# One transpose instead of four for a block's softmax shifts, spread over the query tiles by VectorE with a table

## The chip, the cores and the metric

The kernel runs on one core of a Trainium2 chip. The time is device microseconds of one execution. The kernel before ran three times: 1567.17, 1567.2 and 1570.7 us, median 1567.2. One more execution was profiled: 1566.48 us, with a span of 1564.7 us from the first to the last instruction and a granted TensorE clock of 0.998.

Engine names: PE is TensorE (PEld its weight loads), DVE is VectorE, ACT is ScalarE, POOL is GpSimd, SP issues most DMAs.

## What is computed

A parallel transformer block over `x` of shape (2, 1024, 1024) in float32: the input, plus causal attention with linear position biases, plus a linear layer with binarized weights, both on the normalized input.

```
xn = layernorm(x)
q, k, v = split(clip(xn @ Wqkv.T, -8, 8));  q, k = layer_norm(q), layer_norm(k)   # with weight and bias
scores = q k^T / sqrt(32) + slope[h] * (key_pos - query_pos),  causal mask         # 32 heads of 32
attn = softmax(scores) v @ Wout.T
ffn  = xn @ (mean|W| * sign(W)).T + bias
out  = x + attn + ffn
```

## The kernel before

**Blocks of attention.** The unit of attention is a block (b, qb, g): one of two batches, one of two halves of 512 queries (NQ = 4 tiles of 128), one of eight groups of G = 4 heads. That makes 32 blocks. The four heads of a group lie on partitions 0, 32, 64 and 96 on, so four matmuls, one for each 32 rows of the array, run side by side.

**Two passes over the scores.** The first pass (`first_scores`, L1015 to L1053) has queries on the partitions and finds each query's maximum: matmul L1024, then on VectorE L1043, which adds the position table `rel` and reduces to a maximum; a short instruction on the same line reads the accumulated maximum into `mx` and frees the bank. The second pass (`second_scores`, L1075) has keys on the partitions, because its output is the stationary side of the product with the values. Its exponent needs minus the maximum of each query, which now lies along the free dimension. So the maxima have to be turned.

**Turning the shifts** (`shifts`, L1055 to L1073). `mx` is [128 queries of a tile, 4 heads, 4 query tiles]. GpSimd adds the positions (L1059), negates (L1060) and splits the f32 value into three bf16 parts (L1063, L1065): seven operations of 128x16. They are written into `shift_b`, four tiles of [128, 128], in which head j's three parts stand in columns 32j to 32j+2 of the tile. One step later TensorE transposes the four tiles into one bank (L1070), and ScalarE copies that bank out as `rows` (L1072), [128, 512] in bf16: three rows for each head, 512 queries along them. In `second_scores` a second matmul, here called the fold (L1099), adds the rows to the scores: its stationary operand is three rows of ones, its moving operand the three rows of shifts.

After the fold VectorE masks the diagonal (L1118), ScalarE takes the exponential (L1127), GpSimd adds up the parts for the denominator (L1156), and one step later `weigh_values` multiplies by the values (L1167).

**PSUM.** One pool of seven banks (tag `s`) is used in rotation by everything: first scores, second scores, the turned shifts, projections, transposes and denominators. A new user waits until the reader of the bank seven allocations before is done. An eighth bank holds the attention output.

**The rest of the work** is a generator of pieces: projections of k, q and v by a scheme with seven products for eight (`seven`, L411, with evictions by `combine`, L442 and L453 on VectorE, L458 on ScalarE), the binarized layer (L808, eviction L794), the output projection. Between them, side tasks normalize, transpose (L519) and evict (L585 and L546 on ScalarE).

**The order** is written out: the program issues instructions in the order of the main loop (L1249), and each engine runs its queue in that order. Step n does: `first_scores(n)`; the GpSimd half of `shifts` if a block closes; sometimes `divide`; some pieces; `weigh_values` of step n - 10; `second_scores` of step n - 9; then the second half of the shifts of the block that closed one step before; then more pieces. How many pieces a step takes is computed from fixed costs (`time_of`, `share`, `each`), which know nothing of the shifts.

Of the kernel before, what the change touches and what calls it, by code (L numbers as in the profile page):

```python
# [8 lines left out]
FP = mybir.dt.float32  # L9
FR = mybir.dt.float32r  # L10
BF = mybir.dt.bfloat16
AF = mybir.ActivationFunctionType
ALU = mybir.AluOpType
AX = mybir.AxisListType
# [11 lines left out]
def parallel_block_kernel(  # L26
# [36 lines left out]
    nc = tc.nc  # L63
    B, S, D = x.shape
    P = 128
# [4 lines left out]
    G = 4  # L70
    NQB = S // HALF
    NQ = HALF // P
# [12 lines left out]
    const = ctx.enter_context(tc.tile_pool(name="const", bufs=1))  # L85
# [6 lines left out]
    ps_s = ctx.enter_context(tc.tile_pool(name="ps_s", bufs=7, space=bass.MemoryType.PSUM))  # L92
# [6 lines left out]
    ident = const.tile([P, P], FP, tag="ident", name="ident")  # L99
    make_identity(nc, ident)  # L100
    ident_b = const.tile([P, P], BF, tag="ident_b", name="ident_b")
    nc.vector.tensor_copy(ident_b, ident)
    ones_b = const.tile([P, P], BF, tag="ones_b", name="ones_b")
    nc.vector.memset(ones_b, 1.0)
    ones = const.tile([P, HEAD_DIM], FP, tag="ones", name="ones")
    nc.vector.memset(ones, 1.0)
    mean_w = const.tile([P, P], FP, tag="mean_w", name="mean_w")
# [10 lines left out]
    inv_q = const.tile([P, NC], FP, tag="inv_q", name="inv_q")  # L118
    lnp = const.tile([P, 4, NC], FP, tag="lnp", name="lnp")
    lnq = const.tile([P, 2, NC], FP, tag="lnq", name="lnq")  # L120
    shift_b = const.tile([P, NQ, P], BF, tag="shift", name="shift_b")

    def constants():
        for j, src in enumerate((q_w, q_b, k_w, k_b)):
            nc.sync.dma_start(lnp[:, j, :], src)
        yield 0.0

        nc.gpsimd.iota(  # L130
            rel,
            pattern=[[1, S]],
            base=-(S - P),
            channel_multiplier=-1,
            allow_small_or_imprecise_dtypes=True,
        )
        nc.gpsimd.affine_select(
            out=rel,
            in_=rel,
            compare_op=ALU.is_ge,  # L140
            fill=MASKED,
            base=S - P,
            pattern=[[-1, S]],
            channel_multiplier=1,
        )

        nc.gpsimd.memset(behind, 0.0)
        nc.gpsimd.affine_select(
            out=behind,
            in_=behind,  # L150
            compare_op=ALU.is_ge,
            fill=MASKED,
            base=0,
            pattern=[[1, P]],
            channel_multiplier=-1,
        )

        nc.gpsimd.iota(
            pos,
            pattern=[[0, G], [P, NQ]],
            base=-(HALF // 2),
            channel_multiplier=1,
            allow_small_or_imprecise_dtypes=True,
        )

        nc.gpsimd.iota(
            off,  # L170
            pattern=[[P, NO]],
            base=-(NT - NT // NQB) * P - HALF // 2,
            channel_multiplier=1,
            allow_small_or_imprecise_dtypes=True,
        )

        for h in range(N_HEADS):
            if h % 2 == 0:  # L180
                yield 0.0
            nc.gpsimd.tensor_scalar(kpos[:, h, :], off, slopes[h], None, ALU.mult)
            r0 = HEAD_DIM * (h % G)
            nc.gpsimd.memset(
                inv_q[r0 : r0 + HEAD_DIM, h // G : h // G + 1], QK_SCALE / slopes[h]
            )

        for j in range(2):
            nc.vector.tensor_tensor(lnq[:, j, :], lnp[:, j, :], inv_q, ALU.mult)


        nc.gpsimd.memset(shift_b, 0.0)

# [168 lines left out]
    def score_bank(name):  # L364
        return ps_s.tile([P, HALF], FP, tag="s", name=name)
# [4 lines left out]
    def tokens(t):  # L370
        return slice(t * P, (t + 1) * P)
# [683 lines left out]
    def shifts(b, qb, g):  # L1055

        mx = st.pop(("mx", b, qb, g))
        sh = small.tile([P, G, NQ], FP, tag="sh", name=f"sh_{b}_{qb}_{g}", bufs=2)
        nc.gpsimd.tensor_tensor(sh, mx, pos, ALU.add)  # L1059
        nc.gpsimd.tensor_scalar(sh, sh, -1.0, None, ALU.mult)  # L1060
        sb = shift_b.rearrange("p i (j r) -> p j i r", j=G)
        for n in range(3):
            nc.gpsimd.tensor_copy(sb[:, :, :, n], sh)  # L1063
            if n < 2:
                nc.gpsimd.tensor_tensor(sh, sh, sb[:, :, :, n], ALU.subtract)  # L1065
        yield True

        ps = ps_s.tile([P, NQ, P], BF, tag="s", name=f"trs_{b}_{qb}_{g}")
        for i in range(NQ):
            nc.tensor.transpose(ps[:, i, :], shift_b[:, i, :], ident_b)  # L1070
        rows = small.tile([P, HALF], BF, tag="rows", name=f"rows_{b}_{qb}_{g}", bufs=4)
        nc.scalar.copy(rows, ps.rearrange("p i q -> p (i q)"))  # L1072
        st["rows", b, qb, g] = rows  # L1073

    def second_scores(unit):  # L1075
        add_up_parts(st.pop("adds", []))
        name = "{}_{}_{}_{}".format(*unit[0][0], unit[0][1])
        banks = [score_bank(f"s2_{name}_{j}") for j in range(G)]
        c0 = 0
        for block, kt, q0 in unit:  # L1080
            q, k = st[("q",) + block], st[("k",) + block][kt // NQ]
            c1 = c0 + HALF - q0
            for j in range(G):
                r = slice(32 * j, 32 * j + 32)
                nc.tensor.matmul(  # L1085
                    banks[j][:, c0:c1],
                    k[r, tokens(kt % NQ)],
                    q[r, q0:],
                    start=(c0 == 0),
                    stop=False,  # L1090
                )
            c0 = c1
        c0 = 0
        for block, kt, q0 in unit:
            rows = st[("rows",) + block]
            c1 = c0 + HALF - q0
            for j in range(G):
                r = slice(32 * j, 32 * j + 3)
                nc.tensor.matmul(  # L1099
                    banks[j][:, c0:c1],  # L1100
                    ones_b[r, :],
                    rows[r, q0:],
                    start=False,
                    stop=(c1 == HALF or (block, kt, q0) == unit[-1]),
                )
            c0 = c1
        for j in range(G):
            c0, diagonal = 0, []
            for block, kt, q0 in unit:
                if kt >= block[1] * NQ:  # L1110
                    diagonal.append(c0 // P)
                c0 += HALF - q0
            if diagonal:
                at = banks[j].rearrange("p (i q) -> p i q", q=P)
                step = max(diagonal[-1] - diagonal[0], 1)
                at = at[:, diagonal[0] : diagonal[-1] + 1 : step, :]
                mask = behind.unsqueeze(1).to_broadcast([P, len(diagonal), P])
                nc.vector.tensor_tensor(at, at, mask, ALU.add)  # L1118
        parts = []
        for j in range(G):  # L1120
            pT = work.tile([P, HALF], FP, tag="pT", name=f"pT_{name}_{j}", bufs=16)
            c0 = 0
            for n, (block, kt, q0) in enumerate(unit):
                h = block[2] * G + j
                c1 = c0 + HALF - q0
                a = kt - block[1] * NQ + NT - NQ
                nc.scalar.activation(  # L1127
                    pT[:, c0:c1],
                    banks[j][:, c0:c1],
                    AF.Exp,  # L1130
                    bias=kpos[:, h, a : a + 1],
                    scale=slopes[h],
                )
                if j == 0:
                    parts.append((block, kt, q0, []))
                parts[n][3].append(pT[:, c0:c1])
                c0 = c1

        mine = [p for p in parts if p[0] == parts[0][0]]
        waited = st.pop("waiting", [])  # L1140
        st["waiting"] = parts[len(mine) :]
        st["parts", unit[0]] = mine + waited
        if mine[0][1] == 0:
            st[("sum",) + mine[0][0]] = mine[0][3]
            st["adds"] = waited
        else:
            add_up_parts(mine)

    def add_up_parts(parts):

        for block, kt, q0, pT in parts:
            for j in range(G):
                part_sum = st[("sum",) + block][j][:, q0:]
                late = block == blocks[-1] and kt > NT // 2
                eng = nc.vector if late else nc.gpsimd
                eng.tensor_tensor(part_sum, part_sum, pT[j], ALU.add)  # L1156
# [81 lines left out]
    def short_lead(block):  # L1238

        return block[1] == 1 and block[2] == 0  # L1240

    sides.append(constants())
    fill_until(("q", 0))
    for n in range(3):
# [4 lines left out]
    for n in range(steps + 1):  # L1249
# [22 lines left out]
        if 0 <= m < len(second):  # L1272
            second_scores(second[m])
# [62 lines left out]
```

## Time and profile before

| what | value |
|---|---|
| median of three runs | 1567.2 us |
| the profiled execution | 1566.48 us |
| its span | 1564.7 us, clock 0.998 |
| L1070, transposes | 128, mean 221 ns, first at 311.4, last at 1461.3 |
| L1072, ScalarE's copy | 32, 586 to 718 ns |
| L1059, L1060, L1063, L1065 on GpSimd | 32, 32, 96, 64; medians 232, 254, 253, 230 ns |
| L1099, the fold | 768 matmuls, at 512 wide 376 ns |
| L1118, masks | 320; 424 ns at 256 wide, 291 at 128 |

How to read it: the page gives each engine's busy time, then the chain of work that ended last, then groups of instructions by line, engine and operation, with busy time, mean duration of one, and the idle time just before them with what ended it. The timeline lists instructions in order of time: start, duration, engine, line, what it writes and reads; a number in brackets is idle time before it and its releaser. Instructions of one group that follow each other are merged, with x4 for four of them, and their duration is then that of all together.

### The profile page before, as it was taken

The numbers are of one execution on the slowest core, as the hardware profiler recorded it, in microseconds if no ns is written. First come the engines' busy times: TensorE is split into PE (matmuls) and PEld (weight loads), VectorE is DVE, ScalarE is ACT, GpSimd is POOL, SyncE is SP. The second block draws the span as 40 slices with busy tenths as digits, with TensorE's granted clock in tenths as the row PEclk, the third lists the DMA queues.
The fourth block names the chain that finished last, engine by engine and source line by source line (L and its number), as shares of the span: only waits on it lengthen the run. The fifth ranks groups of instructions, "written<-read, shape, count | busy, mean of one in ns | idle before, by whom it ended". The sixth has DMA issues, their size and how long they took to land.

```text
span 1564.7 us, 25362 instructions
## 1 busy us (share of the span) xinstructions
PE 1539.9 (98%) x8452; PEld 678.9 (43%) x8452; DVE 918.8 (59%) x2617; ACT 689.0 (44%) x1427; POOL 969.5 (62%) x1276
## 2 busy tenths in 40 slices
PE   7999999999999999999999999999999999999998
PEld 3444444444444434333333344555655333343333
DVE  7745353767786566656665565666655565565332
ACT  3543331114665645456543365555444343343430
POOL 4473061024674766675676599877788887777661
PEclk9999999999999999999999999999999999999999
DMA  8877354592333754458932377667677233312232
GB/s 303 296 247 264 101 202 154 176 320 83 103 117 96 251 189 149 116 128 250 277 125 106 140 239 232 142 140 164 140 164 204 80 88 95 88 38 65 58 78 54
DMA packets 117426, 244.94 MB, mean 157 GB/s; under 512 B 10544, under 2 KB 50992, under 8 KB 113968
## 3 DMA queue, kind: packets, MB, share of 16 engines
q1 hardware_dynamic: 90912, 148.94, 28.6%
q0 software_dynamic: 26384, 94.38, 23.5%
q8 instruction: 67, 1.10, 0.3%
q14 instruction: 63, 0.52, 0.1%
HBM read 155.47 MB, written 107.74 MB: 168 GB/s over the span
## 4 chain that ended last, share of the span: by engine, by line
PE 89%; DVE 3%; DMA 2%; POOL 2%; ACT 2%; issue 1%; SPq 0%; POOLq 0%; DVEq 0%; ACTq 0%
PE s L1024 10%; PE s L1085 10%; PE o L1167 8%; PE mm_f L808 8%; PE mm_q_t L411 7%; PE mm_o_t L411 7%; PE mm_v_t L411 7%; PE mm_k_t L411 6%; PE mm_q L411 6%; PE mm_o L411 5%; PE mm_v L411 5%; PE mm_k L411 4%; PE den L1186 2%; PE s L1099 2%; PE tr_k L519 1%
## 5 line engine op out<-in xcount | busy, mean ns | idle before, releaser
L1156 POOL TENSOR_TENSOR pT<-pT,pT 128x512 f32<-128x512 f32 (+3 forms) x628 | 578.2, 980 | 173.3 <-ACT pT L1127 152.3
L1127 ACT ACTIVATE pT<-s,kpos 128x512 f32<-128x512 f32 (+3 forms) x768 | 378.4, 590 | 435.7 <-DVE s L1118 259.3
L1043 DVE CUSTOM_DVE_ANT_0 sumss<-s,rel 128x512 f32<-128x512 f32 (+2 forms) x284 | 179.1, 631 | 104.9 <-PE s L1024 72.9
L1085 PE MATMUL s<-qg,kg 32*128 32x512 f32 (+3 forms) x1536 | 183.7, 520 | 0.6 <-DVE mx L1043 0.6
L1024 PE MATMUL s<-kg,qg 32*128 32x512 f32 (+3 forms) x1536 | 179.6, 521 | 0.2
L1167 PE MATMUL o<-pT,vg 128*32 128x512 f32 (+3 forms) x1536 | 155.5, 494 | 1.2 <-ACT pT L1127 1.2
L808 PE MATMUL mm_f<-sg,hl 128*128 128x512 f32 x512 | 127.0, 399 | 2.1 <-DVE mx L1043 2.1
L1085 PEld LDWEIGHTS s<-qg,kg 32*128 32x128 f32 x1536 | 75.9, 183 | 103.4 <-issue 53.9
L1024 PEld LDWEIGHTS s<-kg,qg 32*128 32x128 f32 x1536 | 73.4, 183 | 105.2 <-issue 46.8
L1118 DVE TENSOR_TENSOR s<-s,behind 128x256 f32<-128x256 f32 (+1 forms) x320 | 96.7, 371 | 35.4 <-PE s L1099 35.2
L411 PE MATMUL mm_o_t<-w_o_t,ot 128*128 128x512 f32 x256 | 116.6, 602 | 0.0
L411 PE MATMUL mm_k_t<-w_k_t,xT 128*128 128x512 f32 x224 | 109.4, 613 | 1.2 <-POOL xT L400 0.8
L411 PE MATMUL mm_q_t<-w_q_t,xp 128*128 128x512 f32 x224 | 108.1, 605 | 0.0
L808 PEld LDWEIGHTS mm_f<-sg,hl 128*128 128x128 f32 x512 | 93.5, 188 | 33.0 <-DVE mx L1043 11.7
L411 PE MATMUL mm_v_t<-w_v_t,xp 128*128 128x512 f32 x224 | 106.3, 606 | 0.1
L411 PE MATMUL mm_k<-w_k,xT 128*128 128x512 f32 x192 | 91.3, 612 | 0.3 <-ACT xT L546 0.3
L411 PE MATMUL mm_v<-w_v,xp 128*128 128x512 f32 x192 | 89.6, 604 | 0.0
L411 PE MATMUL mm_q<-w_q,xp 128*128 128x512 f32 x192 | 88.7, 603 | 0.0
L411 PE MATMUL mm_o<-w_o,ot 128*128 128x512 f32 x192 | 87.7, 602 | 0.0
L1167 PEld LDWEIGHTS o<-pT,vg 128*32 128x32 f32 x1536 | 37.2, 108 | 113.2 <-issue 94.9
L1043 DVE CUSTOM_DVE_ANT_0 umss<-s,rel 128x512 f32<-128x512 f32 x100 | 69.2, 692 | 26.9 <-PE s L1024 16.1
L411 PEld LDWEIGHTS mm_o_t<-w_o_t,ot 128*128 128x128 f32 x256 | 46.7, 190 | 62.5 <-issue 52.7
(224 smaller groups left out, 1985.4 us busy)
## 6 DMA issues: line engine op xcount, KB each, us to landing
xp<-xd SPq DMA_DIRECT2D x16, 1792.0 KB, 8.3
kg<-kd SPq DMA_DIRECT2D x48, 256.0 KB, 4.7
vg<-vd SPq DMA_DIRECT2D x48, 256.0 KB, 5.7
wd_ot<-in_wout_t_dram POOLq DMA_DIRECT2D x11, 1024.0 KB, 9.5
xd<-xT POOLq DMA_DIRECT2D x8, 1280.0 KB, 5.6
x<-in_x_dram SPq DMA_DIRECT2D x16, 512.0 KB, 5.8
kd<-kT POOLq DMA_DIRECT2D x16, 512.0 KB, 4.4
qd<-qT POOLq DMA_DIRECT2D x16, 512.0 KB, 3.9
```

Of the source, the lines that this page charges most:

```text
L411: nc.tensor.matmul(ps, pr[:, FACTOR[block], c, :], W[what, block, c], start=(c == 0), stop=(c == NI - 1),)
L519: nc.tensor.transpose(ps[:, j, :], src[:, (c0 + j) * P : (c0 + j + 1) * P], ident)
L808: nc.tensor.matmul(ps, hl[c // NI][:, m % 2, c % NI, :].bitcast(FR), sg[n, c], start=(m == 0), stop=(m == 2 * NC - 1),)
L1024: nc.tensor.matmul(banks[j][:, c0 : c0 + n], q[r, tokens(i - block[1] * NQ)], k[r, :n], start=True, stop=True,)
L1043: nc.vector.tensor_tensor_reduce(out=sums[:, :n], in0=banks[j][:, c0 : c0 + n], in1=rel[:, o0 : o0 + n], scale=1.0, scalar=m if opened els ...
L1085: nc.tensor.matmul(banks[j][:, c0:c1], k[r, tokens(kt % NQ)], q[r, q0:], start=(c0 == 0), stop=False,)
L1099: nc.tensor.matmul(banks[j][:, c0:c1], ones_b[r, :], rows[r, q0:], start=False, stop=(c1 == HALF or (block, kt, q0) == unit[-1]),)
L1118: nc.vector.tensor_tensor(at, at, mask, ALU.add)
L1127: nc.scalar.activation(pT[:, c0:c1], banks[j][:, c0:c1], AF.Exp, bias=kpos[:, h, a : a + 1], scale=slopes[h],)
L1156: eng.tensor_tensor(part_sum, part_sum, pT[j], ALU.add)
L1167: nc.tensor.matmul(po[32 * j : 32 * j + 32, q0:], v[:, kt % NQ, 32 * j : 32 * j + 32], pT[j], start=(kt == 0), stop=(last is not None and ...
L1186: nc.tensor.matmul(ps[32 * j : 32 * j + 32, :], ones, total[j], start=True, stop=True,)
```

## The change

`shift_b` becomes one tile of [128, 128]. In each head's 32 columns it now holds twelve values: the high parts of the four query tiles, then the middle parts, then the low ones. GpSimd does not negate any more, and writes the low part straight from the subtraction, so five operations are left. One transpose turns everything. A row of the result belongs to one query tile: row r of the bank to tile r mod 4. VectorE reads the bank four times over (the tile dimension is broadcast), multiplies by a table `mine_q` of ones and zeros, which keeps in the columns of tile t only the rows of tile t, and writes `rows`. The fold then takes twelve rows and a stationary operand of minus one. `mine_q` is made once from the identity. ScalarE's copy is gone.

```diff
-    ones_b = const.tile([P, P], BF, tag="ones_b", name="ones_b")
-    nc.vector.memset(ones_b, 1.0)
+    minus_b = const.tile([P, P], BF, tag="minus_b", name="minus_b")
+    nc.vector.memset(minus_b, -1.0)
...
-    shift_b = const.tile([P, NQ, P], BF, tag="shift", name="shift_b")
+    shift_b = const.tile([P, P], BF, tag="shift", name="shift_b")
+    mine_q = const.tile([P, NQ], FP, tag="mine_q", name="mine_q")
...
         nc.gpsimd.memset(shift_b, 0.0)
+
+        nc.vector.tensor_reduce(
+            out=mine_q,
+            in_=ident.rearrange("p (c t) -> p t c", t=NQ),
+            op=ALU.add,
+            axis=AX.X,
+        )
...
         sh = small.tile([P, G, NQ], FP, tag="sh", name=f"sh_{b}_{qb}_{g}", bufs=2)
+        sb = shift_b.rearrange("p (j r) -> p j r", j=G)
+        high, mid, low = (sb[:, :, n * NQ : (n + 1) * NQ] for n in range(3))
         nc.gpsimd.tensor_tensor(sh, mx, pos, ALU.add)
-        nc.gpsimd.tensor_scalar(sh, sh, -1.0, None, ALU.mult)
-        sb = shift_b.rearrange("p i (j r) -> p j i r", j=G)
-        for n in range(3):
-            nc.gpsimd.tensor_copy(sb[:, :, :, n], sh)
-            if n < 2:
-                nc.gpsimd.tensor_tensor(sh, sh, sb[:, :, :, n], ALU.subtract)
+        nc.gpsimd.tensor_copy(high, sh)
+        nc.gpsimd.tensor_tensor(sh, sh, high, ALU.subtract)
+        nc.gpsimd.tensor_copy(mid, sh)
+        nc.gpsimd.tensor_tensor(low, sh, mid, ALU.subtract)
         yield True
 
-        ps = ps_s.tile([P, NQ, P], BF, tag="s", name=f"trs_{b}_{qb}_{g}")
-        for i in range(NQ):
-            nc.tensor.transpose(ps[:, i, :], shift_b[:, i, :], ident_b)
+        ps = ps_s.tile([P, P], BF, tag="s", name=f"trs_{b}_{qb}_{g}")
+        nc.tensor.transpose(ps, shift_b, ident_b)
         rows = small.tile([P, HALF], BF, tag="rows", name=f"rows_{b}_{qb}_{g}", bufs=4)
-        nc.scalar.copy(rows, ps.rearrange("p i q -> p (i q)"))
+        nc.vector.tensor_tensor(
+            rows.rearrange("p (t q) -> p t q", q=P),
+            ps.unsqueeze(1).to_broadcast([P, NQ, P]),
+            mine_q.unsqueeze(2).to_broadcast([P, NQ, P]),
+            ALU.mult,
+        )
...
-                r = slice(32 * j, 32 * j + 3)
+                r = slice(32 * j, 32 * j + 3 * NQ)
                 nc.tensor.matmul(
                     banks[j][:, c0:c1],
-                    ones_b[r, :],
+                    minus_b[r, :],
                     rows[r, q0:],
```

## The prediction

> **What bounds the kernel.** I read the engine shares first, then the chain of work that ended last, then the groups with different shapes kept apart, and last the timeline around each of the 32 places where a block's shifts are turned.
>
> ```profile
> PE 1539.9 (98%) x8452; PEld 678.9 (43%) x8452; DVE 918.8 (59%) x2617; ACT 689.0 (44%) x1427; POOL 969.5 (62%) x1276
> ...
> PE 89%; DVE 3%; DMA 2%; POOL 2%; ACT 2%; issue 1%; SPq 0%; POOLq 0%; DVEq 0%; ACTq 0%
> ```
>
> TensorE is busy for 98% of the span and makes up 89% of the chain. So only TensorE time counts, and other engines count where TensorE waits for them. A busy TensorE also hides short waits, because matmul ends are modelled, so a share alone decides nothing; each place has to be looked at.
>
> The rows that the change touches or resembles (busy us, mean ns of one, idle before):
>
> ```profile
> L1118 DVE TENSOR_TENSOR s<-s,behind 128x256 f32<-128x256 f32 x192 | 68.3, 424 | 24.7 <-PE s L1099 24.6
> ...
> L1072 ACT COPY rows<-trs 128x512 bf16<-128x512 bf16 x32 | 20.1, 627 | 16.3 <-PE trs L1070 16.3
> ...
> L442 DVE TENSOR_TENSOR u_o<-mm_o_t,u_o 128x512 f32<-128x512 f32 x24 | 16.6, 692 | 61.5 <-PE mm_o_t L411 61.5
> ...
> L1070 PE MATMUL trs<-ident_b,shift_b 128*128 128x128 bf16 x128 | 12.7, 221 | 2.1 <-POOL shift_b L1063 2.1
> ...
> L1060 POOL TENSOR_SCALAR sh<-sh 128x16 f32<-128x16 f32 x32 | 8.1, 253 | 2.9
> ```
>
> **TensorE: 96 transposes fewer.** Each block loses three of its four transposes. A record lasts 221 ns, but records overlap: the timeline shows the four together in 0.40 us, so three steps and one record make 0.40, and a step is (0.40 - 0.22) / 3 = 0.06 us. The starts say it more closely: at 1274.85 the first begins, at 1275.08 the matmul behind the four, so 0.23 / 4 = 0.057. I take 0.056, so 0.17 us a block and 96 x 0.056 = 5.4 us in all. That is the upper end from this edit: it counts only where what comes next isn't waiting for something else.
>
> The Trainium skill, page "TensorE: Matmul & The Clock Gate", section on the PE-mode transpose, gives about 275 ns for a bf16 128x128 transpose within a kernel. By it the edit would remove 96 x 275 ns = 26.4 us, an estimate; the steps of 57 ns between starts say that a train of transposes doesn't pay that each, so the sum doesn't use it.
>
> **Where the 0.17 us survives.** I went through the blocks by the time of their first transpose (us from the span's start).
>
> First, the matmul behind the transposes writes the next of seven rotating score banks, which is free only after VectorE has read the third head's row maximum from it (L1043).
>
> ```profile
> 1274.85 0.40 PE L1070 MATMUL trs<-ident_b,shift_b 128*128 128x128 bf16 x4
> 1274.94 0.08 DVE L1043 DVE_READ_ACCUMULATOR2_ANT mx<- 128x1 f32 x1
> ...
> 1275.08 0.69 PE L411 MATMUL mm_o_t<-w_o_t,ot 128*128 128x512 f32 x1
> ```
> ```profile
> 1325.62 0.40 PE L1070 MATMUL trs<-ident_b,shift_b 128*128 128x128 bf16 x4
> ...
> 1325.90 0.08 DVE L1043 DVE_READ_ACCUMULATOR2_ANT mx<- 128x1 f32 x1
> 1326.03 0.30 PEld L411 LDWEIGHTS mm_o_t<-w_o_t,ot 128*128 128x128 f32 x2 [0.19 <-DVE mx L1043]
> ```
>
> In the second the load says that it waits for VectorE; the read ends at 1325.98 and the matmul starts about 0.06 later. In the first there is no wait, but the read ends at 1275.02 and the matmul starts at 1275.08, the same 0.06 behind: both limits coincide. Transposes that end sooner gain nothing in either. The maxima that VectorE is working through were started by L1024, ahead of the transposes, so they do not move. Such blocks: waiting at 357, 984, 1000, 1024, 1040, 1064, 1326, 1420; just touching at 1080, 1180, 1275, 1369. Twelve blocks, gain 0. At 311 the matmul waits 0.28 us for ScalarE's copy of the bank before (L458): gain 0 too.
>
> Second, in the early half little fill stands between the transposes and the next first_scores, which wants the banks that ScalarE's exponentials have yet to read:
>
> ```profile
> 535.27 3.03 ACT L1127 ACTIVATE pT<-s,kpos 128x384 f32<-128x384 f32 x8 [2.66 <-DVE s L1118]
> ...
> 537.21 0.70 PEld L1024 LDWEIGHTS s<-kg,qg 32*128 32x128 f32 x6 [0.76 <-ACT pT L1127]
> ...
> 538.35 0.29 PEld L1024 LDWEIGHTS s<-kg,qg 32*128 32x128 f32 x2 [0.44 <-ACT pT L1127]
> ```
>
> The exponentials end at 538.30 and the last loads go at 538.35. They were released by folds and masks that come before the transposes, and the removed copy (L1072) stands behind them, so nothing here moves. Such blocks: 377, 423, 451, 469, 535, 586, 645, 696, 755, 806, 865, 915. Their eight or sixteen first_scores matmuls take 0.06 to 1.4 us longer from first to last start than the shortest of the same shape (0.55 and 0.77). I give all twelve 0; in the three with 0.06 (645, 696, 865) the wait is there already, so an earlier start only lengthens it.
>
> Free: 328, 406, 941, 1135, 1461. Five x 0.17 = **0.85 us**.
>
> **GpSimd: seven operations become five.** The negation (L1060) and the last cast go. Starts in the train are 0.29 to 0.34 us apart; at 958.20 the seven begin and end at 960.34; with two fewer they end 0.64 us sooner. It matters where TensorE waits for them:
>
> ```profile
> 960.09 0.25 POOL L1063 CAST shift_b<-sh 128x16 bf16<-128x16 f32 x1
> ...
> 960.40 0.40 PE L1070 MATMUL trs<-ident_b,shift_b 128*128 128x128 bf16 x4 [1.52 <-POOL shift_b L1063]
> ```
>
> At 960 the wait falls from 1.52 to about 0.9, and nothing is late behind it: 0.64 + 0.17 = **0.81 us**. At 1232 the wait of 0.6 goes, but then the bank of the first case binds: its read ended at 1231.40, so the matmul starts at 1231.46 instead of 1231.92: **0.46 us**. Elsewhere GpSimd is 3 to 16 us ahead of the transposes. The other 30 blocks relieve it of 0.64 each with nobody waiting: taken as 0.
>
> **VectorE: a product more.** 512 elements out of PSUM with an SBUF table: no row has just this, with bf16 in and out. L442 (692 ns) is nearest; L1118 grows from 291 (128 wide) to 424 (256 wide), which carried on gives an estimate of 690 for 512. I take 0.69 us; the ends are ScalarE's 0.59 for the shortest copy of the same tile and 1.0 for the one cast to bf16 of the start (L102, 998 ns). 32 x 0.69 = 22 us on an engine at 59%. It stands in the queue behind the masks (L1118) and ahead of the next eviction. Queued behind it are that eviction and the next maxima, and TensorE waits for the banks they free. What hides it:
>
> ```profile
> 1135.54 1.42 DVE L1118 TENSOR_TENSOR s<-s,behind 128x256 f32<-128x256 f32 x4
> 1139.20 0.69 DVE L794 TENSOR_TENSOR fo<-mm_f,alpha_bias 128x512 f32<-128x512 f32 x1 [2.24 <-PE mm_f L808]
> ```
>
> VectorE is idle 2.24 us right where the product goes; at the other places from 984 on this gap is 1.55 to 6.3 us, and in most early blocks an idle stretch of 0.7 us or more follows after a few instructions. The wait for the transposes is no new one: they run before the masks end. Packed are 311, 328 and 755: between 0 and 0.69 each if the cover is gone, at most 2.1 us. I take 0: their next bank waits have other releasers (exponentials, ScalarE's copies).
>
> **ScalarE: a copy less.** 20 us go, but the copy stood behind the exponentials and ahead of work with slack. Where ScalarE has no idle stretch behind it (451, 469) up to 0.63 each could come back: 0 to 1.3 us, taken 0. The rows themselves are wanted two steps later or more, so either engine is in time.
>
> **The fold with twelve rows.** No row has twelve. A bf16 weight load of 3 rows takes 93 ns (L1099), of 128 rows 97 ns (L1070), and the 512-wide f32 matmul takes 613 ns with 128 rows (L411) and 640 with 32 (L1085): the row count doesn't set the time. Taken 0; the upper end is 4 ns for each of 768 loads, four side by side, 0.8 us; no reason for a gain. The table mine_q is one VectorE operation near 39 us; 0 taken, 1.0 at most (the cast's 998 ns).
>
> **Sum.** 0.85 + 0.81 + 0.46 = 2.1 us. The profiled execution took 1566.48 (span 1564.7), so 1564.4 of it; it lies 0.7 under the median 1567.2, and from the median I get **1565.1**. A measurement of this kernel tells about 0.3% (4.7 us) from no change.
>
> **Rivals.** (1) All of it comes through: banks and exponentials move up because VectorE's and ScalarE's queues shift too. 5.4 + 2 x 0.64 = 6.7, so 1560.5. For it: TensorE is the bound over the whole; against it: the twenty-five coinciding waits above. (2) Slower: the product delays VectorE's evictions and maxima, and the seven banks come free 0.69 late. It decides where less than 0.69 us of idle time lies between the masks and the next reader of a bank that TensorE wants; if that were so in half the blocks, 16 x 0.69 = 11.0 less 2.1 gives 1576. For it: TensorE's loads waited for L1043 more often than for any other VectorE work, and 357 to 469 and 755 are dense; against it: the gaps shown. (3) Each transpose costs its whole record, as in a train that cannot overlap: 96 x 0.221 = 21 us, 1546. The overlapping starts speak against it.
> By the 275 ns of the Trainium skill (same page and section) this third one would be 1541, an estimate; the trace's steps of 57 ns disagree.
>
> **Numbers.** Forecast 0.68 (all of it within 0.3%), rival 1 0.18, rival 2 0.12, rival 3 0.02. Faster 0.20, within 0.3% 0.68, slower 0.12. The range takes rival 1 and ScalarE's 1.3 below (1559), and above the packed VectorE places, fold and table (2.1 + 0.8 + 1.0) with some of the 3.5 us by which the runs of before differ: 1571.
>
> **What would show it.** Right: the matmul behind the single transpose starts 0.06 after L1043's third read in the twelve blocks; first_scores still ends with the exponentials; the wait at 960 falls to about 0.9 and that at 1232 goes; VectorE's new row reads 0.69 with idle time behind it. Wrong: L442 or L1043 late after the product with TensorE waiting for it, a fold over 376 ns at 512 wide, or a product well over 0.69.

## The result and the profile after

The changed kernel takes 1562.33 us (median of seven runs, 1557.92 to 1564.13), the kernel before beside it 1567.32 us (seven runs, 1566.36 to 1571.02). The ratio is 0.9957, with a 95% interval of 0.9941 to 0.9972: 0.43% faster, about 5 us, where 2.1 us were forecast. The time lies in the range. The likeliest case, a change within 0.3%, did not come (the interval runs from 0.28% to 0.59% faster), and the experiments below show that the larger part of the gain comes from places that the prediction priced at nothing.

The profiled execution took 1562.7 us, with a span of 1560.9 us (before: 1566.48 and 1564.7) and a mean granted clock of 0.995 (before: 0.998). The page of the kernel after, engine shares and chain:

```profile
PE 1534.9 (98%) x8356; PEld 672.9 (43%) x8356; DVE 937.5 (60%) x2650; ACT 673.7 (43%) x1395; POOL 948.1 (61%) x1212
...
PE 72%; DVE 3%; issue 1%; POOL 1%; DMA 1%; ACT 1%; SPq 0%; POOLq 0%; DVEq 0%; ACTq 0%
```

There are 96 matmuls, 32 ScalarE operations and 64 GpSimd operations fewer, and 33 VectorE operations more (32 products and the table). TensorE is still the bound. The shares that the chain names add up to 79% of the span here and to 99% before, so 72% for TensorE against 89% is no reading of the change. The groups of the kernel after, shapes kept apart (busy us, mean ns of one, idle before):

```profile
L1111 PE MATMUL s<-rows,minus_b 12*128 12x512 bf16 x384 | 47.0, 377 | 0.0
...
L1079 DVE TENSOR_TENSOR rows<-trs,mine_q 128x512 bf16<-128x512 bf16 x32 | 21.8, 682 | 2.1 <-PE trs L1077 2.1
...
L1077 PE MATMUL trs<-ident_b,shift_b 128*128 128x128 bf16 x32 | 7.4, 230 | 0.8 <-POOL shift_b L1073 0.7
...
L1073 POOL TENSOR_TENSOR shift_b<-sh,shift_b 128x16 bf16<-128x16 f32 x32 | 7.1, 221 | 2.6
...
L1070 POOL CAST shift_b<-sh 128x16 bf16<-128x16 f32 x32 | 6.3, 196 | 2.1
```

The product takes 682 ns (forecast 690). The fold at 512 wide takes 377 ns with twelve rows (376 with three). The place at 1275 of before, now with one transpose, from the timeline (start, duration, engine, line, what it writes and reads):

```profile
1271.95 0.23 PE L1077 MATMUL trs<-ident_b,shift_b 128*128 128x128 bf16 x1
1272.05 0.08 DVE L1051 DVE_READ_ACCUMULATOR2_ANT mx<- 128x1 f32 x1
...
1272.18 0.70 PE L419 MATMUL mm_o_t<-w_o_t,ot 128*128 128x512 f32 x1
```

The transpose starts 0.10 us before the read of the maximum, the next matmul 0.05 us after the end of that read. Three transposes are gone and the matmul goes no earlier: the coinciding limits were read rightly. The place at 960.40 of before, where TensorE waits for GpSimd:

```profile
954.77 0.22 POOL L1073 TENSOR_TENSOR shift_b<-sh,shift_b 128x16 bf16<-128x16 f32 x1
...
955.05 0.23 PE L1077 MATMUL trs<-ident_b,shift_b 128*128 128x128 bf16 x1 [0.75 <-POOL shift_b L1073]
```

The wait fell from 1.52 to 0.75 us (forecast 0.9). At 1232 of before GpSimd's wait is gone and the bank of VectorE's read takes its place, as forecast:

```profile
1228.56 0.23 PE L1077 MATMUL trs<-ident_b,shift_b 128*128 128x128 bf16 x1
1228.83 0.08 DVE L1051 DVE_READ_ACCUMULATOR2_ANT mx<- 128x1 f32 x1
1228.97 0.30 PEld L419 LDWEIGHTS mm_o_t<-w_o_t,ot 128*128 128x128 f32 x2 [0.32 <-DVE mx L1051]
```

And the block at 535 of before, where nothing was to move:

```profile
533.94 3.03 ACT L1139 ACTIVATE pT<-s,kpos 128x384 f32<-128x384 f32 x8 [2.66 <-DVE s L1130]
...
534.74 0.68 DVE L1079 TENSOR_TENSOR rows<-trs,mine_q 128x512 bf16<-128x512 bf16 x1
...
535.88 0.70 PEld L1032 LDWEIGHTS s<-kg,qg 32*128 32x128 f32 x8 [0.76 <-ACT pT L1139]
```

Before, six weight loads of first_scores went at 1.94 us behind the first exponential and the last two at 3.08, behind all eight exponentials. Now all eight go at 1.94 and are done at 536.58, while the exponentials run on until 536.97. So TensorE no longer waits for the last head's exponentials. That is the unforecast gain.

**Where the time went, block by block.** I matched the matmuls of the two traces one by one in their order, transposes left out, and took for each of the 32 places how much the distance between them changes from the transposes to the end of the next first_scores (us; names are the times in the kernel before):

| places | forecast | measured |
|---|---|---|
| 311, 984 to 1080, 1180, 1275, 1326, 1369, 1420: bank of a maximum or a copy | 0 | 0.00 to 0.04 either way |
| 328, 406, 941, 1135, 1461: free | -0.85 in sum | -0.17, -0.17, -0.17, -0.18, -0.17 |
| 960, GpSimd | -0.81 | -0.94 |
| 1232, GpSimd, then a bank | -0.46 | -0.46 (at the next matmul) |
| 377, 423, 451, 469, 535, 586, 755, 806: exponentials | 0 | -0.72, -0.73, -0.58, -0.73, -0.73, -0.72, -0.72, -0.72 |
| 645, 696: exponentials | 0 | -0.01, -0.01 |
| 865, 915: exponentials | 0 | -0.23, -0.17 |
| 357 | 0 | +1.10, a longer stretch at half clock |

The eight places in the fourth row make 5.7 us. Without 357 all places together make 8.3 us. Part of this is given back by the granted clock: the stretch at half clock behind 357 is longer, and a new one begins at 967.5. The lead of the trace after over that of before was 5.5 us at 960, 2.0 behind that stretch, and 3.3 at the last matmul. That nearly adds up: 8.3 less 1.1 at 357, less 3.5 at 967.5, less 0.5 by which the trace after was behind at 60 us (nearly all of it by 28 us, before the table is made at 40.8), is 3.2.

### The profile page after: what moved, and what is told of

Its sections match the earlier page's. It is cut to its first block, busy times and chain, and to the rows that moved or that the text cites. A ratio compares the mean times of both kernels' runs of the same rounds, so it can differ in the third digit from the quotient of the medians.

```text
span 1560.9 us, 25071 instructions
## 1 busy us (share of the span) xinstructions
PE 1534.9 (98%) x8356; PEld 672.9 (43%) x8356; DVE 937.5 (60%) x2650; ACT 673.7 (43%) x1395; POOL 948.1 (61%) x1212
## 4 chain that ended last, share of the span: by engine, by line
PE 72%; DVE 3%; issue 1%; POOL 1%; DMA 1%; ACT 1%; SPq 0%; POOLq 0%; DVEq 0%; ACTq 0%
PE s L1097 10%; PE s L1032 10%; PE o L1179 8%; PE mm_f L816 8%; PE mm_o_t L419 7%; PE mm_o L419 5%; PE mm_v_t L419 4%; PE mm_q_t L419 4%; PE mm_k_t L419 4%; PE mm_q L419 3%; PE mm_v L419 3%; PE den L1198 2%; PE s L1111 2%; PE mm_k L419 2%; DMA vd<-vraw 1%
## 5 line engine op out<-in xcount | busy, mean ns | idle before, releaser
L1032 PE MATMUL s<-kg,qg 32*128 32x512 f32 (+3 forms) x1536 | 176.2, 523 | 0.1
```

The costliest lines, as they stand in the source:

```text
L1032: nc.tensor.matmul(banks[j][:, c0 : c0 + n], q[r, tokens(i - block[1] * NQ)], k[r, :n], start=True, stop=True,)
```

## The experiments

**Theory.** The gain at the eight places comes from the bank of the turned shifts. It is now read out by VectorE behind the masks, and no longer by ScalarE behind the exponentials. So it comes free sooner and goes to the next first_scores in place of the last bank of the second scores that first_scores used to need (the last head's at five of the eight places, the third head's at 377, 755 and 806). **Rivals:** the three transposes, the two GpSimd operations, or ScalarE's queue made shorter by a copy.

The times of all runs. Each ratio is to the kernel before on the same chip, with its 95% interval:

| run | median us | ratio | interval |
|---|---|---|---|
| after | 1562.33 | 0.9957 | 0.9941 to 0.9972 |
| e1_copy_on_vector | 1561.08 | 0.9954 | 0.9941 to 0.9968 |
| e2_spread_on_scalar | 1569.29 | 1.0008 | 0.9999 to 1.0017 |
| e3_four_transposes | 1562.29 | 0.9958 | 0.9945 to 0.9972 |
| e4_seven_on_gpsimd | 1561.00 | 0.9956 | 0.9942 to 0.9970 |
| e5_product_twice | 1566.19 | 0.9987 | 0.9978 to 0.9996 |
| e6_fold_32_rows | 1560.51 | 0.9955 | 0.9941 to 0.9968 |
| e7_late_release | 1567.58 | 0.9996 | 0.9984 to 1.0008 |
| e8_four_in_one_block | 1561.50 | 0.9958 | 0.9943 to 0.9974 |
| e9_more_fill_behind | 1563.45 | 0.9970 | 0.9960 to 0.9980 |
| e10_most_fill_behind | 1584.44 | 1.0105 | 1.0088 to 1.0123 |

**e1: the kernel before, with only the copy moved to VectorE.** Four transposes, seven GpSimd operations and the fold with three rows stay.

```diff
-        nc.scalar.copy(rows, ps.rearrange("p i q -> p (i q)"))
+        nc.vector.tensor_copy(rows, ps.rearrange("p i q -> p (i q)"))
```

> The kernel before with one edit: VectorE instead of ScalarE copies the turned shifts out; four transposes, seven GpSimd operations and three rows stay. Bank theory (what the forecast missed: the bank of the shifts now comes free in VectorE's queue, so it is handed out again before the last banks of the exponentials, and the next first_scores waits for one exponential pair less): eight early blocks (377 to 806) gain 0.56 us each, so about 4.5 us less than before, 1562.8, and no gain at 960 or 1232. TensorE theory (the gain is the transposes and the GpSimd operations alone): no change, 1567.3 within 1 us.

Measured: 0.9954, as much as the whole change as far as the intervals tell, from this one line. Place by place it is 5.7 of the 8.3 us: the same eight places gain 0.58 to 0.73 us each, as much as in the kernel after; the free places, 960 and 1232 stay within 0.05. Its timeline around 535:

```profile
535.06 1.84 ACT L1127 ACTIVATE pT<-s,kpos 128x128 f32<-128x128 f32 x5
...
535.82 0.69 PEld L1024 LDWEIGHTS s<-kg,qg 32*128 32x128 f32 x8 [0.76 <-ACT pT L1127]
```

Eight loads in one go, with none of the new transposes, products or tables.

**e2: the kernel after, but ScalarE spreads the shifts** with four scaled copies in place of VectorE's product.

```diff
-        nc.vector.tensor_tensor(
-            rows.rearrange("p (t q) -> p t q", q=P),
-            ps.unsqueeze(1).to_broadcast([P, NQ, P]),
-            mine_q.unsqueeze(2).to_broadcast([P, NQ, P]),
-            ALU.mult,
-        )
+        for t in range(NQ):
+            nc.scalar.activation(
+                rows[:, tokens(t)], ps, AF.Copy, scale=mine_q[:, t : t + 1]
+            )
```

> The changed kernel, but ScalarE instead of VectorE spreads the bank, in four activations scaled by a column of mine_q each; one transpose and five GpSimd operations stay. Its banks are handed out as in the kernel before. Bank theory: the eight early blocks gain nothing, 960 gains 0.94, 1232 0.46, the free blocks 0.17 each: 2.1 to 2.7 us less than before, 1565. TensorE theory: all of the gain of the changed kernel stays, about 5 us, 1562.3.

Measured: 1.0008, no gain. The eight places are back within 0.08 us of before; the savings of the one transpose and of GpSimd are there (0.14 to 0.17 at five places, 1.37 at 960, 0.41 at 1232), but 941 lost 0.94, and two stretches of 6.8 us at half clock stand against one of 3.4 of before (both have one more, of 4 to 5 us, at the end). So the total of e2 says little, and the places decide. Its timeline at the block of 535:

```profile
538.58 3.03 ACT L1137 ACTIVATE pT<-s,kpos 128x384 f32<-128x384 f32 x8 [2.66 <-DVE s L1128]
...
540.53 0.70 PEld L1032 LDWEIGHTS s<-kg,qg 32*128 32x128 f32 x6 [0.76 <-ACT pT L1137]
...
541.45 1.19 ACT L1080 ACTIVATE rows<-trs,mine_q 128x128 bf16<-128x128 bf16 x4
541.66 0.29 PEld L1032 LDWEIGHTS s<-kg,qg 32*128 32x128 f32 x2 [0.44 <-ACT pT L1137]
```

Six loads, then two behind the last exponential: the picture of before, with the read of the shifts at its old place.

**e3: the kernel after, with the one transpose done four times** into the same place.

```diff
-        nc.tensor.transpose(ps, shift_b, ident_b)
+        for _ in range(NQ):
+            nc.tensor.transpose(ps, shift_b, ident_b)
```

> The changed kernel with its one transpose done four times into the same place. Bank theory: what the forecast counted for the free blocks comes back, 6 x 0.17 = 1.0 us over the changed kernel, and the eight early gains of about 0.56 stay. TensorE theory: 96 x 0.056 = 5.4 us over the changed kernel, which is the time of before.

Measured: 0.9958. The eight places keep their 0.58 to 0.74, the free ones fall back to 0, and 960 gains 0.75 instead of 0.94. So the 96 transposes are worth 0.17 at seven places (the five free ones, 865 and 915) and 0.19 at 960: 7 x 0.17 + 0.19 = 1.4 us. At the eight places they are worth nothing: the gain there is the same with four transposes as with one. What e3 still gains over before at 960 (0.75) and at 1232 (0.46 at the next matmul) is GpSimd's part, 1.2 us.

**e4: the kernel after, with seven operations on GpSimd.**

```diff
-        nc.gpsimd.tensor_copy(high, sh)
+        for _ in range(3):
+            nc.gpsimd.tensor_copy(high, sh)
```

> The changed kernel with the first cast on GpSimd done three times, so seven operations. Both theories: the wait at 960 is 0.64 us longer again and the matmul behind the transposes at 1232 comes 0.46 us later, 1.1 us over the changed kernel; a theory in which GpSimd's relief of 20 us matters elsewhere gives more than that.

Measured: 0.9956. Apart from 357, which the half clock covers, only 960 (0.41 instead of 0.94) and 1232 (0.37 instead of 0.42, to the end of first_scores) change: 0.6 us for the two operations. That is half of GpSimd's 1.2 us, since the seven end sooner than the seven of before (median 1.88 us against 2.16): these casts are shorter, see below.

**e5: the product twice.**

```diff
-        nc.vector.tensor_tensor(
+        for _ in range(2):
+            nc.vector.tensor_tensor(
```

> The changed kernel with VectorE's product done twice into the same rows. It prices the product and delays the bank's release by one product; in the compiled program 12 instead of 29 of the next first_scores take the bank of the shifts. Bank theory: part of the eight early gains goes, 1 to 4.5 us over the changed kernel. Cover theory (VectorE has idle time behind the masks and only the product's length matters): 0 to 2 us over it. A theory in which VectorE binds: 32 x 0.69 = 22 us over it.

Measured: 0.9987, about 3.9 us over the kernel after for 32 x 0.69 = 22 us more on VectorE. At 377, 535, 586, 755 and 806 the gain is gone; at 423, 451 and 469 0.48 to 0.66 of it stay. Five lost gains are 5 x 0.72 = 3.6 us, nearly all that the second product costs, and the bank that comes free 0.69 later explains them (see the banks below). Of the rest, 915 gains 0.57 more than in the kernel after, and 1040 loses 0.33. VectorE's load as such is covered.

**e6: the fold with all 32 rows** of a head's tile; rows 12 to 31 are zeros.

```diff
-                r = slice(32 * j, 32 * j + 3 * NQ)
+                r = slice(32 * j, 32 * j + 32)
```

> The changed kernel with the fold over all 32 rows of a head (rows 12 to 31 are zeros). If the row count costs nothing, the fold's records and the steps between their starts stay as they are and the time is that of the changed kernel within 1 us. If rows cost, the 20 more rows show it: 768 weight loads of up to 4 ns more, four side by side, 0.8 us.

Measured: 0.9955, the matmul at 512 wide 374 ns, the weight load 93 ns. The rows cost nothing.

**e7: the kernel after, with one more small read of the shifts' bank on ScalarE**, behind the product. The product, the single transpose and the five operations stay.

```diff
+        late = small.tile([P, 1], FP, tag="late", name=f"late_{b}_{qb}_{g}", bufs=2)
+        nc.scalar.copy(late, ps[:, 0:1])
```

> The changed kernel, with one ScalarE copy of a single column of the shifts' bank added behind the exponentials, so that the bank comes free in ScalarE's queue while VectorE still does the product. Banks are handed out nearly as in the kernel before. Bank theory: the eight early gains go, about 4.5 us over the changed kernel, little under before. Engine theory (ScalarE's queue is relieved of 0.63 us a block, and that is the gain): nearly all stays, since this copy is 0.2 us, so 1 to 2 us over the changed kernel.

Measured: 0.9996, the gain is gone. The eight places are back at 0, and 645 and 696 lose 0.72 each. The forecast gains are still there (0.17 to 0.18 at the five free places, 0.99 at 960, 0.41 at 1232), so what went is the gain from the bank. Its timeline at the block of 535:

```profile
536.98 3.02 ACT L1141 ACTIVATE pT<-s,kpos 128x384 f32<-128x384 f32 x8 [2.66 <-DVE s L1132]
...
537.79 0.68 DVE L1079 TENSOR_TENSOR rows<-trs,mine_q 128x512 bf16<-128x512 bf16 x1
...
538.92 0.70 PEld L1032 LDWEIGHTS s<-kg,qg 32*128 32x128 f32 x6 [0.76 <-ACT pT L1141]
...
539.84 0.21 ACT L1086 CAST late<-trs 128x1 f32<-128x1 bf16 x1
...
540.05 0.29 PEld L1032 LDWEIGHTS s<-kg,qg 32*128 32x128 f32 x2 [0.43 <-ACT late L1086]
```

The product is done at 538.47 as in the kernel after, but ScalarE reads the bank once more at 539.84, and the last two loads go at 540.05. The trace names the small read as their releaser, since it ends just then. By the banks in the program they wait for the last head's exponential, which ended at 540.00, and they go 0.05 behind it, as they did before (538.30 and 538.35). A releaser is inferred from times, so where two end together the banks decide.

**The banks.** Each compiled program says which bank a tile lies in, and so who had it before. These are the former tenants of the four banks of the next first_scores; `s2 j` is head j of the second scores, `trs` the turned shifts:

```
block (batch, half, group)   before                     after
(0,0,7)                      s2 0  s2 1  s2 2  s2 3      s2 0  s2 1  trs   s2 2
(0,0,3), behind one mm_k     s2 0  s2 1  s2 2            s2 0  s2 1  trs
(0,1,4), behind one mm       s2 0  s2 1  s2 2            s2 0  s2 1  trs
```

In the last two rows the first entry of four is that projection's bank, the other three are shown. The next first_scores gets the bank of the shifts in 1 of the 32 blocks before, in 29 after, 29 in e1, e3, e4, e6 and e8, 1 in e2, 12 in e5, 0 in e7. So the seven banks are not used in rotation, as the kernel's description and the prediction had it. Their order was settled when the program was built, and it changed with the place of the bank's last reader. That it follows the order in which the banks are reckoned to come free fits all nine programs (before, after, e1 to e7); it is inferred from them. Of the 29 blocks only those gain where the bank that is no longer needed was the wait that ended last. At 645 and 696 the bank of the shifts takes the place of a projection's bank, the third head's exponentials are awaited as before, and nothing is gained; in e7 first_scores there gets the last head's bank, which it did not before, and loses 0.72. e5 sorts itself in the same way: at 423, 451 and 469 first_scores still gets the bank of the shifts in place of the last head's and keeps its gain; at 535 and 586 it gets both, at 377, 755 and 806 it doesn't get it, and the gain is gone.

**e8: four transposes in the block at 357 alone.** This asks whether three missing transposes make the stretch at half clock behind 357 longer.

```diff
-        nc.tensor.transpose(ps, shift_b, ident_b)
+        for _ in range(NQ if (b, qb, g) == (0, 0, 2) else 1):
+            nc.tensor.transpose(ps, shift_b, ident_b)
```

> The changed kernel with four transposes in the block at 357 alone. It asks whether fewer transposes there keep TensorE's granted clock at half for two stretches of 3.4 us instead of one. If so, the stretch behind 357 is 3.4 us as in the kernel before, and the granted clock of the runs is 0.997 or more, 1.7 us less than the changed kernel; if the length is chance, the stretch is 6.8 again, and the time that of the changed kernel within 1 us.

Measured: the stretch is 6.8 us again, and the time 0.9958. Four transposes there don't bring the 3.4 us back.

**e9 and e10: more fill behind the second scores.** `BEFORE` is the share of a step's fill pieces that stands ahead of the second half of the step. With less ahead, more stands between the transposes and the next first_scores, so that the exponentials have time to end.

```diff
-    BEFORE = 0.4
+    BEFORE = 0.25
```

> The changed kernel with a quarter instead of two fifths of a step's fill ahead of second_scores (BEFORE 0.25), so more fill stands between the transposes and the next first_scores while the exponentials read their banks. In the changed kernel first_scores still loses 10.1 us to such waits over the whole span. Bank theory: some of it goes, 1 to 5 us under the changed kernel, unless the banks behind weigh_values now come late instead. A theory without these waits expects no difference from the changed kernel.

> The same with a tenth of the fill ahead (BEFORE 0.1). Bank theory: first_scores waits still less, but weigh_values and second_scores follow first_scores sooner and find VectorE still reading the maxima; between 4 us under and 8 us over the changed kernel. A theory without such waits expects no difference.

Measured: 0.9970 with 0.25 and 1.0105 with 0.1, neither better than the kernel after. What first_scores takes from first to last start over the shortest of its shape, added up over all 144 of them, falls from 11.4 us in the kernel after to 4.5 in e9 (15.3 in the kernel before; the expectation had 10.1 for the kernel after), but another wait grows. It stands in the waits of TensorE's loads (us in total, times, longest), in the kernel after, in e9 and in e10:

```profile
PEld s L1097 <- DVE mx L1051: 32.3, 54, 1.2
```
```profile
PEld s L1097 <- DVE mx L1051: 42.8, 66, 1.5
```
```profile
PEld s L1097 <- DVE mx L1051: 52.8, 84, 2.0
```

The second scores come sooner behind the first and want the banks that VectorE's maxima still hold. The wait moves from one reader of the banks to another. e10 also ran at half clock in six stretches and one at the end. No run is faster than the kernel after by more than the intervals, and e1 and the kernel after can't be told apart.

## Why the prediction was right in its range and wrong in its size

**Right.** The places that wait for a maximum's bank and the one at 311 give nothing (357 can't be read, the half clock covers it): limits that coincide, or nearly, hide an edit of 0.17 us. The five free places give 0.85 as forecast. At 960 the gain is 0.94 against 0.81, since the five GpSimd operations take 1.36 us (median) and not the 1.5 that fewer starts alone would leave. At 1232 it is 0.46, as worked out. The product (682 ns against 690) and the fold (377 against 376 ns) were sized rightly. "VectorE is idle where the product goes" holds: a second product costs what it takes from the bank order, not 22 us.

**Wrong: "the removed copy (L1072) stands behind them, so nothing here moves".** For eight of the twelve places with exponentials that is the failed step: 5.7 us instead of 0. The facts in it were right: the last loads went with the last exponential that they needed, and the copy stood behind that. But it priced the copy's *time* and not the *bank* that it held. With "the next of seven rotating banks" the bank that first_scores gets would be fixed whatever its readers do. It is handed out by another order, and a reader that moves from behind the exponentials to ahead of their end changes who gets which. e1 shows that the move of the read suffices, e7 that a late read undoes it. Also wrong, by 0.2 each, are 865 and 915: an earlier start there did come through.

**The rivals.** Rival 1 said that banks move up because the queues shift. That is close to what happened, yet its sum was of other terms: 5.4 us of transposes and 1.3 of GpSimd. The transposes gave 1.4 (e3 against the kernel after) and GpSimd 1.2 (e3 against before), and 5.7 came from a term that neither it nor the forecast had. Its time (1560.5) is near the measured one with the wrong content. So it is luck in part that the time lies in the range: the range was drawn down to 1559 for rival 1, and not for the bank. Rival 2, the product delaying VectorE's evictions, did not come in the kernel after; in e5 a mechanism like it takes 3.9 us, through five places and not sixteen. Rival 3 is refuted by e3: 96 transposes more leave the median where it was (1562.29 against 1562.33).

The Trainium skill, page "TensorE: Matmul & The Clock Gate", section on the PE-mode transpose, gives about 275 ns for such a transpose. By it, taken as the cost of each, e3 would have been 96 x 275 ns = 26 us slower, an estimate; where the difference of e3 shows, it is 0.17 us for three, 57 ns each.

**What is left.** Forecast and the eight places make 2.1 + 5.7 = 7.8 us, with 865 and 915 8.2; 5.0 were measured between medians. In the two profiled executions the stretches at half clock take most of the rest, as added up above. For the medians that is only argued, from the granted clocks of the runs, next.

## What to carry to other kernels

When a reader of a PSUM bank moves to another engine, ask first what stands ahead of it in the old queue and in the new one: that sets when the bank comes free, and so which tenant the next matmul waits for. Take the banks from the program and not from a count of allocations, and compare them before and after the edit. And fewer instructions on the engine that bounds the whole give time only at the places where no other wait ends with them: here 1.4 us of the 5.4.

## What the hardware showed that was not expected

**The clock halves in stretches, and a run's time goes with them.** TensorE's granted clock falls to half in stretches of 3.4 or 6.8 us: in the profile of before at 357.7 for 3.4, in that of after at 356.5 and 967.5 for 6.8 each, and in both for 4 to 5 us at the end. Two windows of after, around these stretches (stretch, length, then busy time of PE, PEld, DVE, ACT, POOL with counts, PEclk as the granted clock, DMA share, GB/s):

```profile
340.00:380.00 40.00, 39.09 (x194) 16.57 (x194) 25.72 (x82) 11.39 (x24) 14.30 (x25) 0.91 0.40 149
955.00:1000.00 45.00, 41.89 (x304) 23.55 (x305) 26.55 (x90) 17.67 (x37) 40.79 (x51) 0.92 0.61 157
```

and the same of before:

```profile
340.00:380.00 40.00, 38.41 (x203) 16.60 (x203) 26.18 (x84) 12.64 (x27) 16.20 (x30) 0.96 0.41 152
955.00:1000.00 45.00, 42.50 (x331) 23.78 (x329) 26.26 (x94) 19.29 (x39) 42.95 (x60) 1.00 0.68 182
```

Clock 0.91 and 0.92 against 0.96 and 1.00. The seven runs of the kernel after follow their mean clock: 1562.7 and 1564.1 us at 0.995, 1563.2 at 0.996, 1560.9 and 1562.3 at 0.997, 1557.9 and 1558.6 at 0.999. 0.004 of 1560 us is 6 us, the whole spread. So a single run of this kernel carries a chance part as large as the change itself, and the intervals above are the measure of it. At equal clock (0.997) before took 1567 to 1569.7 us, after 1560.9 to 1562.3, and e7 1567.3 to 1567.9: the conclusions stand there too.

What starts a stretch stays open in part. Ahead of 967.5 TensorE, in the kernel after, waited longer than before:

```profile
963.61 1.12 PE L746 MATMUL ps_a<-alpha_bias,mean_w 128*128 128x512 f32 x2
966.63 1.25 PE L746 MATMUL ps_a<-alpha_bias,mean_w 128*128 128x512 f32 x2 [1.89 <-ACT pT L1139]
967.82 2.62 PE L1032 MATMUL s<-kg,qg 32*128 32x512 f32 x8
```

The same place before:

```profile
970.82 1.12 PE L738 MATMUL ps_a<-alpha_bias,mean_w 128*128 128x512 f32 x2 [0.56 <-ACT pT L1127]
```

That is 1.89 us of idle time against 0.56; the eight matmuls behind it then take 2.62 us. Behind 353 there is no such gap: TensorE runs matmuls of 32-row tiles with waits of 0.2 to 0.4 us (its records cover 3.05 of the 3.42 us ahead of 356.5), and the clock halves all the same. The Trainium skill, page "TensorE: Matmul & The Clock Gate", section "What's actually happening", has the clock at half after an idle window of about 3.4 us. The lengths here, 3.4 and 6.8 us, agree with that window; that TensorE must be idle for all of one does not hold in these traces, and the measurement decides. Why the stretch behind 357 differs is not settled. It is 3.4 us in the three profiles with four transposes throughout (before, e1, e3); with one transpose it is 6.8 in after, e2, e4, e5 and e7, 3.4 in e9, and missing in e6. e8, with four in that block alone, has 6.8, which speaks against the transposes of that block.

**GpSimd's small casts depend on where they write.** The cast of 128x16 to bf16 took 253 ns into single places 32 or 128 columns apart, and 196 ns into groups of four neighbours. That is 0.06 us for each cast. It is most of the reason why the seven of e4 took 1.88 us against 2.16 before: e4 has four of the short casts where before had three of the long ones and a negation of 254 ns, 0.23 of the 0.28 us.
